# Layer 2's raw attention weights issued on ScalarE's queue instead of SyncE's

## The chip, the core and the metric

The kernel runs on one core of a Trainium2 chip. A core has five engines that run their own instruction streams in order: TensorE (PE, with its weight loads shown as PEld), VectorE (DVE), ScalarE (ACT), GpSimd (POOL) and SyncE (SP), which computes nothing here and only issues transfers. ACT and POOL can issue transfers as well. The metric is the time of one execution on the device in microseconds (us); the kernel before took 1427.58 us in the median of three runs (1425.8 to 1429.04).

## The reference

Four layers work on x of shape (4, 256, 256); each adds a cross-attention and then a feed-forward part to x, both on a layer-normalised copy. All is in float32. What bears on this change is the end of layer 1 and the beginning of layer 2.

Layer 1's feed-forward part is a mixture of experts. Each of the 1024 tokens picks two of eight experts, and a shared expert runs for all tokens:

```python
    scores = jax.nn.softmax(logits, axis=-1)
    topk_w, topk_idx = jax.lax.top_k(scores, K)
    ...
    g = jax.nn.silu(jnp.einsum('th,efh->tef', x, w_gate)) * jnp.einsum('th,efh->tef', x, w_up)
    expert_out = jnp.einsum('tef,ehf->teh', g, w_down)
    y = jnp.einsum('te,teh->th', cw, expert_out).reshape(b, s, h)
    y = y + _swiglu_mlp(x, sw_gate, sw_up, sw_down).reshape(b, s, h)
```

Layer 2's attention has 16 query heads of 128 over 8 key and value heads, with weights Wq (256, 2048), Wk and Wv (128, 1024) and Wo (2048, 256):

```python
    q = (text_hidden @ Wq).reshape(B, T_text, N_HEADS, HEAD_DIM).transpose(0, 2, 1, 3)
    k = (vision_tokens @ Wk).reshape(B, T_vis, N_KV_HEADS, HEAD_DIM).transpose(0, 2, 1, 3)
    v = (vision_tokens @ Wv).reshape(B, T_vis, N_KV_HEADS, HEAD_DIM).transpose(0, 2, 1, 3)
    ...
    return out @ Wo
```

## The kernel before

The program is one straight line of instructions. Inside a stretch marked `manual_schedule`, PE, ACT, DVE and POOL take their instructions in the order of the source. SP's instructions, nearly all transfers, are put in order by the planner.

**Layer 1's experts.** Tokens are sorted by expert into 23 blocks of 128 slots (`NBLK`). The loop at lines 2464 to 2492 is a pipeline over these blocks, three deep. For block j it does, on the engines in brackets:
- `gather` [POOL]: bring the block's 128 token rows from `xd` in HBM into `xg` by an indirect transfer; there are four buffers, so POOL runs up to four blocks ahead.
- `turn_in` [PE, ACT]: transpose into PSUM (`pxg`, L2344), then ACT copies to `xgT` (L2346).
- `weights` [DVE]: copy the expert's weights into `we`.
- `rise` [PE, ACT, DVE]: twelve matmuls into `pgu` (L2369), two Silu on ACT into `sg` (L2374, L2375), two products on DVE into `gT` and `gR`.
- `fall` and `last_rows` [PE]: matmuls into `pyr` (L2387, L2393).
- `store` [ACT, SP]: ACT scales `pyr` into the result tile `yr` (L2398); SP then stores `yr` to `yd` in HBM, 128 KB (L2401). There are three `yr` buffers, so the `yr` of block j can be written only when the store of block j - 3 has landed.

Blocks go in pairs: `last_rows` and `store` of both are done in the odd iteration. On ACT the two `yr` are followed by the next iteration's `xgT`, its two `sg`, another `xgT` and two more `sg`, and then the next two `yr`.

After the loop the tokens' results are gathered back from `yd` by POOL (L2410).

**Layer 2's folding.** Before layer 2's attention the weights are folded: Wq with Wk, and Wv with Wo, in eight steps (`folding`, matmuls `pm` at L985 and `pn` at L1001), two for each of four groups of raw weights. A group is four transfers, 512, 128, 128 and 512 KB (`load_raw`, L969). They are issued within the block loop, after blocks 1, 5, 9 and 13. The first group goes into parts of the folded weights' own tiles that are written last (so the profile calls these transfers `n_sb` and `m_sb`), the other three into tiles of a pool with three buffers. `done["slots"]` is the last `yr` instruction; `behind` makes the load wait for it:

```python
    dma = nc.sync.dma_start(dst, src[a * P : (a + z) * P, :].rearrange("(h e) d -> e h d", e=P))
    if after:
        behind(dma, after)
```

SP's order in the loop is so: the stores of two blocks, a group of four loads, the stores of two blocks and two more, a group of loads, and so on. Layers 1 and 3 load their raw weights by the same function, with SP as the issuer.

Of the kernel before, what the change touches and what calls it, by code (L numbers as in the profile page):

```python
# [17 lines left out]
P = 128  # L18
# [817 lines left out]
def bounded_path(ctx: ExitStack, tc: tile.TileContext, t, out: bass.AP, over):  # L836


    nc = tc.nc
# [38 lines left out]
    def behind(dma, ins):  # L878

        tc.add_manual_dep(  # L880
            dma.ins, ins.name, mybir.DependencyInfo(mybir.DependencyClass.Sync, mybir.DependencyReason.DATA),
            reason="pace",
        )
# [71 lines left out]

    raws = {}

    def load_raw(L, i, after=None, tiles=None):

        wq, wk, wv, wo = (t[f"L{L}_{n}"] for n in ("wqT", "wkT", "wvT", "wo"))  # L960
        h0, g0 = 4 * i, 2 * i
        if tiles is None:
            tiles = [
                rawp.tile(shape, F32, tag=f"{n}_t", name=f"{n}_{L}_{i}")
                for n, shape in (("wq", [P, 4, D]), ("wk", [P, 2, DC]), ("wv", [P, 2, DC]), ("wo", [P, 4, D]))
            ]
        wq_t, wk_t, wv_t, wo_t = tiles
        for dst, src, a, z in ((wq_t, wq, h0, 4), (wk_t, wk, g0, 2), (wv_t, wv, g0, 2), (wo_t, wo, h0, 4)):
            dma = nc.sync.dma_start(dst, src[a * P : (a + z) * P, :].rearrange("(h e) d -> e h d", e=P))  # L969
            if after:  # L970
                behind(dma, after)
        raws[L, i] = wq_t, wk_t, wv_t, wo_t

    def folding(L, m_sb, n_sb):

        for i in range(4):
            h0 = 4 * i
            if (L, i) not in raws:
                load_raw(L, i)
            wq_t, wk_t, wv_t, wo_t = raws.pop((L, i))  # L980
            for g in range(2):
                pm = bank("mm", [P, ND, 2, DC], f"pm_{L}_{i}_{g}")
                for d in range(ND):
                    for h in range(2):
                        nc.tensor.matmul(  # L985
                            pm[:, d, h, :],
                            lhsT=wq_t[:, 2 * g + h, d * P : (d + 1) * P],
                            rhs=wk_t[:, g, :],
                            start=True,
                            stop=True,  # L990
                        )
                h1 = h0 + 2 * g
                nc.scalar.mul(m_sb[:, :, h1 : h1 + 2, :], pm, 1.0 / math.sqrt(P))
                m2 = rawp.tile([P, ND, 2, DC], F32, tag="m2", name=f"m2_{L}_{i}_{g}", bufs=1)
                for h in range(2):
                    nc.scalar.activation(
                        m2[:, :, h, :], m_sb[:, :, h1 + h, :], AF.Square,
                        accum_out=msq[:, L - 1, h1 + h : h1 + h + 1],
                    )
                pn = bank("mm" if "ring" in banks else "os"[g], [P, 2, D], f"pn_{L}_{i}_{g}")  # L1000
                nc.tensor.matmul(  # L1001
                    pn, lhsT=wv_t[:, g, :], rhs=wo_t[:, 2 * g : 2 * g + 2, :], start=True, stop=True
                )
                nc.vector.tensor_copy(n_sb[:, h1 : h1 + 2, :], pn)
                yield

    def folded(L):
        return (
            mnp.tile([P, ND, H, DC], F32, tag="m_sb", name=f"m_sb{L}"),
            mnp.tile([P, H, D], F32, tag="n_sb", name=f"n_sb{L}"),  # L1010
        )
# [7 lines left out]
    done = {}  # L1019
# [1148 lines left out]
    with tc.manual_schedule(engines={E.PE, E.Activation, E.DVE, E.Pool}):  # L2168
        back = ExitStack()
        backp = back.enter_context(tc.tile_pool(name="back", bufs=4, side="right"))  # L2170
        with tc.tile_pool(name="f1", bufs=2) as fp:
# [292 lines left out]
            for j in range(-2, NBLK + 1):  # L2464
                if j + 2 < NBLK:
                    if j + 2 >= 4:
                        blocks[j + 2].gather()
                    if j >= 0:
                        blocks[j + 2].weights()
                    blocks[j + 2].turn_in()  # L2470
                if 0 <= j + 1 < NBLK:
                    blocks[j + 1].rise()
                if 0 <= j < NBLK:
                    blocks[j].fall()
                    if j % 2 == 0 and j + 1 < NBLK:
                        blocks[j + 1].other_rows()
                    if j % 2 or j == NBLK - 1:
                        pair = blocks[j - j % 2 : j + 1]
                        for one in pair:
                            one.last_rows()  # L2480
                        for one in pair:
                            one.store()

                if j == 1:

                    mn = folded(2)
                    load_raw(
                        2, 0, done["slots"],
                        (mn[1][:, 8:12, :], mn[0][:, 1, 12:14, :], mn[0][:, 1, 14:16, :], mn[1][:, 12:16, :]),
                    )  # L2490
                if j in (5, 9, 13):
                    load_raw(2, j // 4, done["slots"])
            fold = folding(2, *mn)
            backs = {}
            shared[3].up([1, 2])
# [301 lines left out]
    with tc.manual_schedule(engines={E.PE, E.Activation, E.DVE, E.Pool}):  # L2797
# [124 lines left out]
    slots = late.tile([P, KSEL], F32, tag="slots", name="slots")  # L2922
    nc.gpsimd.iota(
        slots, pattern=[[1, KSEL]], base=1, channel_multiplier=0, allow_small_or_imprecise_dtypes=True
# [212 lines left out]
    with tc.manual_schedule(engines={E.PE, E.Activation, E.DVE, E.Pool}):  # L3137
# [34 lines left out]
        a, z = slice(0, P), slice(P, D)  # L3172
# [13 lines left out]
def tile_cross_attention_blocks(tc: tile.TileContext, t, out: bass.AP):  # L3186
    nc = tc.nc
    with tc.tile_pool(name="over", bufs=1) as pool:
        over = pool.tile([1, 1], I32, tag="over", name="over")
        again = bounded_path(tc, t, out, over)  # L3190
        with tc.If(again > 0):
            general_path(tc, t, out)
# [66 lines left out]
```

## Time and profile before

| what | value |
|---|---|
| median of three runs | 1427.58 us (1425.8 to 1429.04) |
| the profiled execution | 1426.74 us, of which the span is 1424.9 |
| granted clock of TensorE, mean | 0.997 |
| PE busy | 1401.6 us, 98% of the span |
| DVE, POOL, ACT busy | 896.7, 679.2, 590.2 us (63%, 48%, 41%) |
| SP's transfer queue | 37.29 MB in all |
| ACT's transfer queue | 1.31 MB: three loads at the start, two stores at the end |
| the block loop's pairs, undisturbed | 4.75 us |

The profile is of one execution. A row names the engine, the line of the source, what is written from what, and how long one instruction took; the idle time of the engine before it is given with what ended it. ACTq and SPq are the queues of an engine's own instructions that only issue transfers: the row's length is how long the issue held the engine's instruction stream, not how long the data took to land. In tables of stretches each engine's busy time in that stretch stands with its number of instructions.

### The profile page before, as it was taken

The numbers are of one execution on the slowest core, as the hardware profiler recorded it, in microseconds if no ns is written. First come the engines' busy times: TensorE is split into PE (matmuls) and PEld (weight loads), VectorE is DVE, ScalarE is ACT, GpSimd is POOL, SyncE is SP. The second block draws the span as 40 slices with busy tenths as digits, with TensorE's granted clock in tenths as the row PEclk, the third lists the DMA queues.
The fourth block names the chain that finished last, engine by engine and source line by source line (L and its number), as shares of the span: only waits on it lengthen the run. The fifth ranks groups of instructions, "written<-read, shape, count | busy, mean of one in ns | idle before, by whom it ended". The sixth has DMA issues, their size and how long they took to land. (4 is left out here: it accounts for less than half of the span.)

```text
span 1424.9 us, 20263 instructions
## 1 busy us (share of the span) xinstructions
PE 1401.6 (98%) x7393; PEld 927.0 (65%) x7393; DVE 896.7 (63%) x2012; ACT 590.2 (41%) x1168; POOL 679.2 (48%) x812
## 2 busy tenths in 40 slices
PE   9999999999999999999999999999999999999998
PEld 7566676566556667887555666665985556666666
DVE  6666863666665557554676565648755666575675
ACT  5667454433433332255443333333454433333331
POOL 3322332475655455231566656566214765445560
PEclk9999999999999999999999999999999999999999
DMA  5000220300000000272120000000331000000000
GB/s 163 2 1 2 75 75 1 86 27 1 8 0 8 1 8 22 53 217 91 49 56 8 16 1 1 8 1 9 117 106 48 16 1 1 1 1 1 1 1 33
DMA packets 49449, 46.82 MB, mean 33 GB/s; under 512 B 8281, under 2 KB 45242, under 8 KB 49340
## 3 DMA queue, kind: packets, MB, share of 16 engines
q1 hardware_dynamic: 45740, 37.29, 8.6%
q0 software_dynamic: 2496, 6.82, 1.8%
q8 instruction: 61, 1.00, 0.3%
q10 hardware_dynamic: 1104, 1.31, 0.3%
q14 instruction: 48, 0.39, 0.1%
HBM read 38.60 MB, written 6.82 MB: 32 GB/s over the span
## 5 line engine op out<-in xcount | busy, mean ns | idle before, releaser
L1870 POOL TENSOR_TENSOR half<-pT 128x1024 f32<-128x1024 f32 x93 | 218.2, 2347 | 290.7 <-ACT pT L1854 215.6
L1851 PE MATMUL ps<-qT,cT 128*128 128x512 f32 x768 | 345.6, 593 | 0.0
L1859 PE MATMUL po<-pT,c_sb 128*128 128x512 f32 x768 | 345.3, 592 | 0.0
L1854 ACT ACTIVATE pT<-ps,mbias 128x512 f32<-128x512 f32 x384 | 263.7, 687 | 155.9 <-PE ps L1851 141.6
L1859 PEld LDWEIGHTS po<-pT,c_sb 128*128 128x128 f32 x768 | 145.8, 190 | 183.2 <-issue 183.2
L1851 PEld LDWEIGHTS ps<-qT,cT 128*128 128x128 f32 x768 | 138.9, 190 | 138.4 <-issue 136.5
L1863 ACT COPY oT<-po 128x512 f32<-128x512 f32 x96 | 56.2, 586 | 265.0 <-PE po L1859 265.0
L1906 POOL TENSOR_TENSOR oT<-oT,wide 128x512 f32<-128x512 f32 x90 | 114.3, 1290 | 17.3 <-DVE wide L1905 17.3
L1831 DVE TENSOR_TENSOR qT<-qT,paq 128x128 f32<-128x128 f32 x90 | 25.4, 283 | 94.9 <-ACT qT L1830 94.9
L1344 ACT ACTIVATE pT<-ps 128x512 f32<-128x512 f32 x128 | 65.9, 604 | 32.6 <-PE ps L1340 32.4
L1878 DVE TENSOR_TENSOR half<-half 128x512 f32<-128x512 f32 x96 | 71.6, 746 | 2.7 <-POOL half L1868 2.5
L1831 DVE TENSOR_TENSOR w<-w,pao 128x128 f32<-128x128 f32 x21 | 6.0, 286 | 106.5 <-ACT w L1830 106.5
L1880 DVE STREAM_TRANSPOSE turned<-half 128x512 f32<-128x512 f32 x96 | 68.3, 712 | 6.3
L1821 PE MATMUL paq<-xnT_a,m_sb 128*128 128x128 f32 x360 | 71.3, 280 | 0.0
L1821 PE MATMUL paq<-xx,m_x 128*128 128x128 f32 x360 | 69.6, 275 | 0.0
L1821 PEld LDWEIGHTS paq<-xnT_a,m_sb 128*128 128x128 f32 x360 | 57.3, 192 | 17.2 <-issue 8.7
L1884 DVE TENSOR_REDUCE sums<-turned 128x16 f32<-128x512 f32 x96 | 65.9, 686 | 3.3
L1821 PE MATMUL pao<-n_x,ox 128*128 128x128 f32 x336 | 65.2, 276 | 0.3 <-POOL ox L1747 0.3
L1830 ACT COPY qT<-paq 128x128 f32<-128x128 f32 x90 | 23.9, 265 | 94.1 <-PE paq L1821 94.1
L1905 DVE STREAM_TRANSPOSE wide<-rz 128x512 f32<-128x512 f32 x96 | 62.2, 685 | 0.1
L1834 DVE TENSOR_TENSOR qT<-qT,pbq 128x384 f32<-128x384 f32 x90 | 49.9, 554 | 9.4
L1821 PEld LDWEIGHTS paq<-xx,m_x 128*128 128x128 f32 x360 | 54.7, 192 | 0.0
(454 smaller groups left out, 2589.2 us busy)
## 6 DMA issues: line engine op xcount, KB each, us to landing
wq<-in_L_wqT SPq DMA_DIRECT2D x11, 512.0 KB, 5.1
wo<-in_L_wo SPq DMA_DIRECT2D x11, 512.0 KB, 7.4
yd<-yr SPq DMA_DIRECT2D x23, 128.0 KB, 4.9
w<-in_F_w SPq DMA_DIRECT2D x4, 512.0 KB, 3.6
xd<-xn_f SPq DMA_DIRECT2D x7, 256.0 KB, 2.2
wk<-in_L_wkT SPq DMA_DIRECT2D x11, 128.0 KB, 5.2
wv<-in_L_wvT SPq DMA_DIRECT2D x11, 128.0 KB, 5.6
x_sb<-in_x SPq DMA_DIRECT2D x4, 256.0 KB, 3.1
```

The costliest lines, as they stand in the source:

```text
L1344: nc.scalar.activation(pT[kp][:, j], ps[j], AF.Exp)
L1821: nc.tensor.matmul(p[:, at, :], lhsT=lhsT, rhs=rhs, start=(k == 0 and at == 0), stop=(k == len(of) - 1 and i == which[-1]),)
L1851: nc.tensor.matmul(ps, lhsT=cT[:, b, k * P : (k + 1) * P], rhs=qT, start=True, stop=True)
L1854: nc.scalar.activation(pT[:, k, :], ps, AF.Exp, bias=mbias[:, b, k : k + 1])
L1859: nc.tensor.matmul(po, lhsT=c_sb[:, b, k, :], rhs=pT[:, k], start=(k == 0), stop=(k == NK - 1))
L1863: done["head"] = nc.scalar.copy(raw, po).ins
L1870: nc.gpsimd.tensor_tensor(half, pT[:, 0:2], pT[:, 2:4], ALU.add)
L1878: nc.vector.tensor_tensor(part, half[:, 0], half[:, 1], ALU.add)
L1880: nc.vector.transpose(turned.rearrange("p f i -> p (f i)"), part)
L1884: nc.vector.tensor_reduce(sums[b, hp // 4][:, hp % 4, :], turned, AX.X, ALU.add)
L1905: nc.vector.transpose(wide, rzs[b, hp // 4][:, hp % 4, :, None].to_broadcast([P, NB, 32]))
L1906: eng.tensor_tensor(outs[b, hp], outs[b, hp], wide.rearrange("p f i -> p (f i)"), ALU.mult)
```

## The change

`load_raw` gets a parameter for the queue that issues its transfers. The four calls in layer 1's block loop, which bring layer 2's raw weights, pass ScalarE; other callers still get SyncE. The transfers themselves, their tiles and the tie to the last `yr` are as before. Since ACT takes its instructions in the order of the source, a group's four issues now stand on ACT behind the two `yr` of blocks 0 and 1 (4 and 5, 8 and 9, 12 and 13) and ahead of the next `xgT`. The stores of `yr` stay on SP.

```diff
-    def load_raw(L, i, after=None, tiles=None):
+    def load_raw(L, i, after=None, tiles=None, queue=None):
...
-            dma = nc.sync.dma_start(dst, src[a * P : (a + z) * P, :].rearrange("(h e) d -> e h d", e=P))
+            dma = (queue or nc.sync).dma_start(dst, src[a * P : (a + z) * P, :].rearrange("(h e) d -> e h d", e=P))
             if after:
                 behind(dma, after)
...
                 if j == 1:
 
                     mn = folded(2)
                     load_raw(
                         2, 0, done["slots"],
                         (mn[1][:, 8:12, :], mn[0][:, 1, 12:14, :], mn[0][:, 1, 14:16, :], mn[1][:, 12:16, :]),
+                        queue=nc.scalar,
                     )
                 if j in (5, 9, 13):
-                    load_raw(2, j // 4, done["slots"])
+                    load_raw(2, j // 4, done["slots"], queue=nc.scalar)
```

## The prediction

> **What bounds the kernel now.** I read the page's slices first, then the busy time of each engine pair by pair of blocks in the stage that the change touches, then the timeline of that stage.
>
> The page (part 2, one digit for each fortieth of the span):
>
> ```profile
> PE   9999999999999999999999999999999999999998
> ACT  5667454433433332255443333333454433333331
> PEclk9999999999999999999999999999999999999999
> ```
>
> PE is busy over 90% in nearly every slice at its full clock, so a us in which PE stands still inside a stage is a us of the span, and nothing later waits for a fixed time that could swallow it. ACT is half idle on average, which says nothing about one moment. The chain that ended last is followed back only to 1060.8 us, behind this stage, so for the stage itself I go by stretches and waits.
>
> Stretches of two blocks each (us and, in brackets, instructions of PE, PEld, DVE, ACT, POOL; then the clock, the DMA share and GB/s):
>
> ```profile
> 607.20:611.95 4.75, 4.75 (x38) 3.98 (x36) 2.59 (x7) 2.56 (x8) 1.91 (x2) 1.00 0.57 123
> 611.95:616.70 4.75, 4.75 (x38) 3.98 (x36) 2.59 (x7) 2.56 (x8) 1.91 (x2) 1.00 1.03 340
> ...
> 635.70:641.40 5.70, 5.00 (x38) 4.01 (x36) 2.54 (x7) 2.57 (x8) 1.91 (x2) 1.00 0.59 142
> 641.40:646.15 4.75, 4.75 (x38) 3.98 (x36) 2.53 (x7) 2.56 (x8) 0.97 (x1) 1.00 0.86 257
> 646.15:652.53 6.38, 5.01 (x38) 4.01 (x36) 2.53 (x7) 2.57 (x8) 0.00 (x0) 1.00 0.38 127
> ```
>
> A pair takes 4.75 us when nothing disturbs it, and PE fills all of it. Two pairs are longer: 5.70 (+0.95) and 6.38 (+1.63). These 2.58 us are all that this stage loses to waits between pairs. The timeline shows why (start, length, engine, line; idle before and its releaser in brackets):
>
> ```profile
> 638.04 0.47 ACT L2398 ACTIVATE yr<-pyr,wslot 128x256 f32<-128x256 f32 x1 [1.75 <-DMA yd<-yr]
> 638.41 0.36 ACT L2346 COPY xgT<-pxg 128x256 f32<-128x256 f32 x1
> 638.83 1.59 PE L2369 MATMUL pgu<-xgT,we 128*128 128x128 f32 x12 [0.70 <-ACT xgT L2346]
> 649.17 0.47 ACT L2398 ACTIVATE yr<-pyr,wslot 128x256 f32<-128x256 f32 x1 [2.43 <-DMA yd<-yr]
> 649.54 0.36 ACT L2346 COPY xgT<-pxg 128x256 f32<-128x256 f32 x1
> 649.96 1.59 PE L2369 MATMUL pgu<-xgT,we 128*128 128x128 f32 x12 [1.37 <-ACT xgT L2346]
> ```
>
> ACT wants to write a result tile yr (three buffers) whose earlier store to yd has not landed. Queued behind it on ACT is the copy xgT, and PE's next pgu needs that. The late stores were issued behind raw weights on the same queue: stores issued at 631.6 and 642.0 took 6.2 and 6.6 us to land, those at 652.7 and 657.7, with no load ahead, 1.8 and 1.7.
>
> These two rows also give a law. The pairs begin (first pxg) at 635.72 and 646.17; xgT starts 2.69 and 3.37 us later, and the pair is 0.95 and 1.63 longer. So a pair loses (start of xgT after the pair's start) minus 1.74 us. In the undisturbed pair at 607.23 xgT starts at 608.06, 0.83 in: ACT has 0.91 us of slack there and no more.
>
> **Part 1, removed: sixteen load issues from SP.** The rows of the first and last group:
>
> ```profile
> 608.71 0.45 SPq L969 DMA_DIRECT2D n_sb<-in_L_wqT  x1
> 609.21 0.54 SPq L969 DMA_DIRECT2D m_sb<-in_L_wkT  x1
> 609.79 0.47 SPq L969 DMA_DIRECT2D m_sb<-in_L_wvT  x1
> 610.30 0.47 SPq L969 DMA_DIRECT2D n_sb<-in_L_wo  x1
> ...
> 638.91 0.60 SPq L969 DMA_DIRECT2D wq<-in_L_wqT  x1
> 639.57 0.50 SPq L969 DMA_DIRECT2D wk<-in_L_wkT  x1
> 640.12 1.16 SPq L969 DMA_DIRECT2D wv<-in_L_wvT  x1
> 641.32 0.61 SPq L969 DMA_DIRECT2D wo<-in_L_wo  x1
> ```
>
> From first start to last end the four groups hold SP for 2.06, 2.02, 2.77 and 3.02 us. Nothing computes on SP, so their removal alone saves nothing; what it may save is the two waits for stores, 2.58 us. I take all of it. The next store pair is issued one pair later, 612.58 against 608.71 for the first load; four issues on ACT will begin 0.4 us earlier than on SP and the pair itself grows by some 1.5 us, so the store comes up to 2 us later relative to the load, with less of the load in front of it. In the last group the gain is larger still: there SP's loads came 3.2 us into the pair, because they stood behind the stalled store, and on ACT they start 1 us in. From below: if a store still takes 6.6 us beside loads, the relief can be 0. A row near that end is the gathers xg, which have POOL's queue to themselves and still land in 3.7 to 6.8 us beside loads, against 2.8 without. But yr has to wait only when a store takes longer than about one pair plus 0.3 us (the 5.1 us landing of the store at 612.6 cost ACT 0.20 and PE nothing), and pairs with loads get longer.
>
> [...]
>
> **Part 2, added: the same sixteen issues on ACT, four at a time, right behind the two yr of a pair.** Behind them on ACT stand xgT, the two sg and the next xgT; PE waits for xgT, DVE's gT for sg. They begin when the second yr has ended, since they are tied to it: 0.95 us into the pair, plus 0.04 as between yr and its store on SP now. The trace shows three issues on ACT of another shape at the start and two at the end:
>
> ```profile
> L865 SPq DMA_DIRECT2D c_sb<-in_ctx x3: 390/409/427, 6.4 to 9.0; - x3
> L865 ACTq DMA_DIRECT2D c_sb<-in_ctx x1: 465/465/465, 0.8 to 0.8; - x1
> ```
>
> Same shape, 0.465 on ACT against 0.409 on SP; the two out stores have medians 0.552 and 0.512. I take ACT as 1.1 times SP. An undisturbed group is 2.04 on SP, so 2.25 on ACT. The two longer groups had 0.7 and 0.95 us more, each with one wv issue of about 1.2 us. I don't see its cause; on ACT's queue no stores stand ahead, so I take half, 2.6 and 2.7. Bounds: below, SP's 2.04 for all; above, 3.02 for all.
>
> By the law, with xgT 0.02 after the last issue, a group of length X costs PE 0.99 + 0.02 + X - 1.74 = X - 0.73 us: 1.52, 1.52, 1.87, 1.97, in all 6.9 us. The breakeven against the 2.58 is X = 1.38, or about 0.31 us an issue; every one of the sixteen rows on SP is 0.38 or more.
>
> **Part 3, moved past.** The stores keep SP's order among themselves and go out no later. POOL's gathers run two pairs ahead (9.5 us) and landed in 6.8 at most: covered by 2.7 us; without that cover pxg would wait. The folding begins at 662.5 with the first group and reaches the fourth at about 676; the last load, issued by about 640 on ACT with at most 7.7 us to landing, is there by 648. If that cover were gone, PE's pm would wait. In the built program of before, each transfer also waits for the one eight issues earlier; for a load that is the load of the group before, two pairs (9.5 us and more) earlier against 7.7: nothing, but on ACT such a wait would hold the whole chain.
>
> **Sum.** +6.9 - 2.58 = +4.3 us. The profiled execution took 1426.74 (span 1424.9 and 1.84 around it) and would take 1431.0; it stood 0.84 below the median of the runs, so for the median I say 1427.58 + 4.3 = 1431.9. A measurement of this kernel can tell about 0.2%, 2.86 us, from no change: the borders are 1424.7 and 1430.4.
>
> **The rivals.**
> - *Issues off PE's path (not slower).* Place: ACT between the second yr and xgT. ACT idles some 2.2 us of each pair, and if four issues took less than 1.38 us there the change would pay; below 0.73 us they cost nothing and the 2.58 are pure gain: 1425.0. Against it: sixteen rows of 0.38 and more. 10 in 100.
> - *Early start.* If the issues needn't wait for the end of the second yr but follow its start (0.48 in, 0.47 earlier), the undisturbed groups cost 1.05 each: 4.2 - 2.58 = +1.6, 1429.2. For it: xgT now starts before the second yr has ended. Against it: the loads are tied to that instruction's completion. 13 in 100.
> - *Long issues.* Every group holds ACT for 3.02 us as the fourth did SP: 4 x 2.29 - 2.58 = +6.6, 1434.2. 14 in 100.
> - *Stores no faster.* The two stalls stay although the queue is their own, as for the gathers: +6.9, 1434.5. 8 in 100.
> - *My forecast*, 55 in 100: from groups of 2.04 (4 x 1.31 - 2.58 = +2.7) to groups of 2.25, 2.25, 3.0 and 3.3, with the full excess (7.9 - 2.58 = +5.3): 1430.3 to 1432.9 as its own range.
>
> Slower by over 0.2%: the forecast but for its lowest edge (0.51) and the two last rivals (0.22), 0.73. Within: that edge (0.04), the early start (0.13) and half of the first rival (0.05), 0.22. Faster by over 0.2% needs a little more than the whole 2.58 us: the other half, 0.05. The range leaves out the first rival, at 1425.0, and a tail above the last two: 1428.5 to 1435.
>
> **What would show it.** Right: ACT issues of 0.4 to 0.6 us in four groups behind yr; the four pairs with loads 6.2 to 6.8 us long, with pgu waiting for xgT about 1.4 us; no ACT wait for yd in the pairs that were 5.70 and 6.38 (the second back at 4.75); stores landing in under 5 us. Wrong: pairs with loads still at 4.75 (issues hidden), a yr still waiting for yd (stores no faster), ACT issues of 1 us (long issues), or a pm that waits for a raw weight.

## The result and the profile after

The changed kernel took 1434.35 us in the median of five runs (1432.61 to 1434.69), the kernel before 1427.58 in five runs beside it (1425.80 to 1429.75): a ratio of 1.004, 95% interval 1.0028 to 1.0051. The profiled execution took 1434.67 us, its span 1432.9, at a mean granted clock of 0.995 against 0.997 before.

The slices of the page say nothing of it: PE is at 9 in all but the last, and the granted clock reads as before:

```profile
PEclk9999999999999999999999999999999999999999
```

The stretches of two blocks, in the columns of before (length; busy us of PE, PEld, DVE, ACT, POOL with their instructions; clock, DMA share, GB/s):

```profile
611.06:617.25 6.19, 5.02 (x39) 4.02 (x37) 2.59 (x8) 2.58 (x8) 1.91 (x2) 1.00 0.70 197
...
643.89:650.40 6.51, 5.02 (x38) 4.02 (x37) 2.58 (x8) 2.58 (x8) 1.91 (x2) 1.00 0.75 201
...
655.15:659.90 4.75, 4.75 (x39) 3.99 (x37) 2.54 (x8) 2.57 (x8) 0.00 (x0) 1.00 0.21 66
```

The first, third, fifth and seventh pair, those with a group of loads, are 1.44, 1.46, 1.45 and 1.76 us longer than 4.75. The others are undisturbed, the ninth (655.15) too, which lost 1.63 before. The timeline of the first and the last group (start, length, engine; idle before and its releaser in brackets):

```profile
611.16 0.84 ACT L2398 ACTIVATE yr<-pyr,wslot 128x256 f32<-128x256 f32 x2 [0.45 <-PE pyr L2393]
612.03 0.41 ACTq L969 DMA_DIRECT2D n_sb<-in_L_wqT  x1
612.49 0.58 ACTq L969 DMA_DIRECT2D m_sb<-in_L_wkT  x1
613.11 0.56 ACTq L969 DMA_DIRECT2D m_sb<-in_L_wvT  x1
613.71 0.48 ACTq L969 DMA_DIRECT2D n_sb<-in_L_wo  x1
614.23 0.37 ACT L2346 COPY xgT<-pxg 128x256 f32<-128x256 f32 x1 [2.22 <-PE pxg L2344]
614.65 1.59 PE L2369 MATMUL pgu<-xgT,we 128*128 128x128 f32 x12 [1.17 <-ACT xgT L2346]
...
645.32 0.98 ACTq L969 DMA_DIRECT2D wk<-in_L_wkT  x1
...
647.81 1.60 PE L2369 MATMUL pgu<-xgT,we 128*128 128x128 f32 x12 [1.49 <-ACT xgT L2346]
```

ACT is not computing between yr and xgT, but it is not free: the four issues fill 612.03 to 614.19. The bracket on xgT, "2.22 <-PE pxg", names the wrong releaser: pxg was there at 611.5, and the issues are what came last. From first start to last end the groups hold ACT for 2.16, 2.17, 2.17 and 2.47 us, the last because one wk issue took 0.98.

What ACT waited for ahead of the 23 yr, in the answer for that tile (us, times), first after, then before:

```profile
  PE pyr L2393: 5.2, 11
  issue: 1.1, 1
```

```profile
  DMA yd<-yr: 4.6, 4
```

The waits for stores, 4.6 us in four places before, are gone; what is left is PE's own pyr and one gap of 1.1 us that stands in both. How long each store took to land is not given in the changed kernel's traces; that no yr waited says that every store was in time.

**The account of the two traces.** From the first pxg of block 0 to the first pm of the folding it is 55.29 us before (607.23 to 662.52) and 58.80 after (611.06 to 669.86): +3.51, which is the 6.11 us that the four pairs are longer, less the 2.60 us that the two no longer lose. Yet the two spans differ by 8.0. Of the rest, 3.83 us was there when block 0 began, ahead of anything the change touches (607.23 against 611.06), and about 0.6 came behind the last matmul. The clock column, third from the end, shows where most of the 3.83 is from, in the stretch 40 to 60 us; before, then after:

```profile
40.00:60.00 20.00, 17.44 (x224) 11.18 (x220) 15.99 (x36) 14.41 (x29) 4.01 (x7) 1.00 0.01 2
```

```profile
40.00:60.00 20.00, 17.44 (x203) 11.30 (x202) 16.90 (x37) 12.98 (x26) 3.58 (x6) 0.91 0.01 2
```

PE is as busy in both, but at a clock of 0.91 instead of 1.00 over 20 us; from 586 to 600 it is 0.76 instead of 0.88. That is 1.8 and 1.7 us of full clock missing. Whether that belongs to the change was the first question to the chip.

### The profile page after: what moved, and what is told of

Read it like the earlier page. It is cut to its first block, busy times and chain, and to the rows that moved or that the text cites. A ratio compares the mean times of both kernels' runs of the same rounds, so it can differ in the third digit from the quotient of the medians.

```text
span 1432.9 us, 20265 instructions
## 1 busy us (share of the span) xinstructions
PE 1405.9 (98%) x7393; PEld 930.5 (65%) x7393; DVE 897.2 (63%) x2012; ACT 591.3 (41%) x1168; POOL 679.9 (47%) x812
```

## The experiments

Beside the times, each run is read by two numbers that the clock elsewhere does not touch: the lengths of its pairs, and the *loop* from block 0's first pxg to the first pm. With every pair at 4.75 the loop is 52.69 us; what a kernel has above that it has lost there.

**The changed kernel again** (no edit).

> The changed kernel once more, unaltered. Its profile put +3.5 us into the block loop (four pairs with loads at 6.19, 6.21, 6.20, 6.51 instead of 4.75, and 2.58 us of waits for stores gone), but it measured +6.8 in the medians. Theory 'clock': the rest is time in which TensorE's clock was granted at half, ahead of the loop, where the instruction streams of the engines are the same; then the loop adds +3.5 again, and what is over varies with the granted clock: a run of clock 0.997 would take about 1431. Rival 'change': the rest belongs to the change; then the total is +6 to +7 again at any clock, and some stretch behind the loop is longer by 3 us.

Measured: 1431.36 us in the median of seven runs (1430.49 to 1434.57) against 1427.23; ratio 1.0034 (1.0018 to 1.0051). The stretch again:

```profile
40.00:60.00 20.00, 17.43 (x224) 11.08 (x220) 16.36 (x36) 14.42 (x29) 4.03 (x7) 1.00 0.01 2
```

The clock is that of the kernel before (and 586 to 600 has 0.88), and block 0 begins at 607.62, 0.39 later than before. Its pairs with loads take 6.16, 6.37, 6.16 and 6.23, the others 4.75; the loop is 58.62. So of the 3.8 us ahead of the loop 3.4 were one execution's clock, and the loop's loss of 6 us (6.11, here 5.93) is the kernel's own.

**Load issues spread on ACT**, one behind each of the next four xgT instead of four in a row.

```diff
+            if later is None:
+                issue()
+            else:
+                later.append(issue)
...
+            slots_left = []
...
                     blocks[j + 2].turn_in()
+                if slots_left:
+                    slots_left.pop(0)()
...
-                        queue=nc.scalar,
+                        queue=nc.scalar, later=slots_left,
```

> The sixteen loads stay on ACT, but one issue stands behind each xgT instead of four behind the second yr, so that they fall into ACT's idle time ahead of sg (0.65 us in the even blocks, 1.01 in the odd ones, against issues of 0.41 to 0.58). Theory 'place': ACT's hold costs only because it stands ahead of xgT; all pairs take 4.75, the +6.1 us of the four long pairs go and the relief of 2.58 stays: 2.6 us below before, 1425.0 (6 below the changed kernel). Rival 'issue': an issue on ACT slows its neighbours wherever it stands (transfers issued there, sixteen times 0.4 us): 1431 or more.

Measured: 1426.20 (1424.37 to 1427.99), ratio 0.9992 (0.9981 to 1.0002). The first issue in ACT's timeline, behind the xgT of 608.65, and the stretch of its pair:

```profile
608.79 0.41 ACTq L970 DMA_DIRECT2D n_sb<-in_L_wqT  x1
```

```profile
607.82:612.57 4.75, 4.75 (x39) 3.99 (x37) 2.83 (x9) 2.56 (x8) 2.08 (x2) 1.00 0.61 190
```

All pairs are 4.75 and the loop is 52.69. The same sixteen issues on the same queue cost PE nothing where each stands in a gap of ACT, so it is the place of the issues, four in a row ahead of xgT, that costs 6 us. No yr waits for a store either.

**Loads on SyncE as before, results in more buffers.** From block 2 on, yr is one of eight slices of a tile that is idle until the folding.

```diff
-                    yr = fp.tile([P, D], F32, tag="yr", name=f"yr{j}", bufs=3)
+                    if j < 2:
+                        yr = fp.tile([P, D], F32, tag="yr", name=f"yr{j}", bufs=3)
+                    else:
+                        yr = mn[0][:, 0, 2 * (j % 8) : 2 * (j % 8) + 2, :].rearrange("p h c -> p (h c)")
```

> The kernel before, with loads on SP, but results from block 2 on are written to eight places in a tile that is idle in the loop (the folded weights' m_sb) instead of three yr tiles. It measures the relief alone. Theory: no yr waits for a store, the pairs of 5.70 and 6.38 become 4.75, and the time falls by 2.6 us to 1425.0. Rival 'late next': the stores' delay shows up elsewhere (the gathers of the results behind the loop wait for the last store) and the gain is under 1 us.

Measured: 1425.61 (1424.31 to 1428.73), ratio 0.9993 (0.9981 to 1.0004); all pairs 4.75, loop 52.68. The pair that took 6.38 before:

```profile
645.20:649.95 4.75, 4.75 (x39) 3.99 (x37) 2.54 (x8) 2.56 (x8) 0.00 (x0) 1.00 0.53 155
```

So the waits for stores are all that the kernel before loses in the loop, and more buffers remove them as fully as the change does.

**The changed kernel without the tie to the last yr.**

```diff
-                        2, 0, done["slots"],
+                        2, 0, None,
...
-                    load_raw(2, j // 4, done["slots"], queue=nc.scalar)
+                    load_raw(2, j // 4, queue=nc.scalar)
```

> The changed kernel, but the loads are not tied to the end of the second yr; their place on ACT is the same. Theory 'early start' as a size: the first issue begins at the second yr's start plus 0.1, some 0.4 us earlier, and each of the four pairs is 0.4 us shorter (about 5.8 instead of 6.2): 1.7 us below the changed kernel. Rival: an issue waits for the running activation anyway and nothing changes (within 0.5 us of the changed kernel).

Measured: 1430.43 (1427.23 to 1433.34), ratio 1.0021 (1.0010 to 1.0032). ACT's timeline at the first group, and at the last pair:

```profile
607.39 0.47 ACT L2398 ACTIVATE yr<-pyr,wslot 128x256 f32<-128x256 f32 x1 [0.45 <-PE pyr L2393]
607.44 0.39 ACTq L969 DMA_DIRECT2D n_sb<-in_L_wqT  x1
...
651.03 0.47 ACT L2398 ACTIVATE yr<-pyr,wslot 128x256 f32<-128x256 f32 x1 [2.15 <-DMA yd<-yr]
```

The issues now start 0.05 us after the first yr, beside the two activations, and a group costs 0.54, 1.24 (its wk issue was slow), 0.64 and 0.60. But a wait for a store is back: the yr at 651.03 needs the store of a yr that ended at 644.1, which so took some 7 us to land, although it had SyncE's queue to itself. That pair lost 1.36. The loop is 57.09. The rival fell, since the issue of 607.44 did not wait for the activation that ran from 607.39. And the own queue did not ensure that a store was in time when the loads ran beside it; it is one store in this trace, the others were in time.

**Six useless copies on ACT instead of the issues**, behind the second yr of blocks 5, 9 and 13; loads on SyncE, results in seven slices as above.

```diff
+                if j in (5, 9, 13):
+                    for _ in range(6):
+                        nc.scalar.copy(mn[0][:, 0, 14:16, :].rearrange("p h c -> p (h c)"), blocks[j].xgT.rearrange("p d t -> p (d t)"))
```

> The loads stay on SyncE and results have their own slices (as in sp_yr8: all pairs 4.75 us, median 1425.61), and ACT instead makes six useless copies of 128x256 behind the second yr of blocks 5, 9 and 13, three pairs in all. Theory 'hold' (a pair loses whatever keeps ACT beyond its slack, transfers have nothing to do with it): with copies of 0.33 to 0.37 us, 2.0 to 2.2 us in all, xgT starts 3.0 to 3.2 us into the pair and each of the three pairs loses 1.25 to 1.45 us: pairs of 6.0 to 6.2, loop +3.8 to +4.4 over sp_yr8, 1429.4 to 1430.0 us. Rival 'transfers' (the long pairs of the changed kernel came from loads and gathers colliding when ACT issues them): pairs stay 4.75 to 4.95 and the time at 1425.6 to 1426.2.

Measured: 1431.27 (1428.19 to 1434.98), ratio 1.0017 (1.0004 to 1.0030). The six copies of the second of the three pairs, and the stretch of the first:

```profile
629.99 2.58 ACT L2489 COPY m_sb<-xgT 128x256 f32<-128x256 f32 x6
```

```profile
618.08:624.41 6.33, 5.01 (x39) 4.01 (x37) 2.59 (x8) 4.79 (x14) 1.92 (x2) 1.00 0.71 203
```

The copies took 2.58 us, more than the 2.0 to 2.2 I had expected, and xgT starts 3.32 us into the pair; 3.32 - 1.74 = 1.58, and the three pairs are 6.33 or 6.34, the others 4.75. The loop, 57.45, lies above the expected range because the copies took longer, and the time does too. Work that moves no data over a queue costs what the issues cost: the hold of ACT is the cause, not the transfers.

**Each load in two halves**, eight issues in a group.

```diff
+            for k in range(2 if queue else 1):
+                n = z // 2 if queue else z
+                dma = (queue or nc.sync).dma_start(dst[:, k * n : (k + 1) * n], part[:, k * n : (k + 1) * n])
```

> The changed kernel with each load cut into two halves: the same bytes, eight issues in a group on ACT instead of four, the first behind the second yr. Theory 'hold per issue': 0.4 to 0.55 us an issue, 3.2 to 4.4 us a group, xgT 4.2 to 5.4 us into the pair, each of the four pairs loses 2.5 to 3.6 us, that is +1.0 to +2.2 over the changed kernel's 1.45; loop +4.2 to +8.7 over the changed kernel, 1435.6 to 1443 us. Rival 'hold per byte' (an issue's length goes with the rows it describes, so halves take half the time): group 2.2 us, pairs 6.2, 1431 to 1432 us as in act_again.

Measured: 1447.35 (1446.80 to 1450.25), ratio 1.0131 (1.0109 to 1.0152), above the range of either theory. The halves take as long to issue as whole loads (eight in 4.01 us at the first group, four whole loads in 2.16), so the hold goes by issues and not by bytes. xgT starts 5.02 us into that pair, which by the law costs 3.28; the pair, 609.92 to 619.58, lost 4.91. Two stretches of it, with the clock third from the end, and PE's row show the rest:

```profile
609.92:615.20 5.28, 2.42 (x20) 2.08 (x18) 0.83 (x2) 1.10 (x3) 1.91 (x2) 1.00 0.66 181
...
616.20:617.20 1.00, 1.00 (x6) 1.00 (x6) 0.94 (x3) 0.00 (x0) 0.00 (x0) 0.50 1.06 367
```

```profile
615.37 2.50 PE L2372 MATMUL pgu<-xgT,we 128*128 128x128 f32 x12 [3.03 <-ACT xgT L2349]
```

PE stood still for 3.03 us, and then its granted clock was halved for 3.4 us: twelve matmuls took 2.50 instead of 1.59. The four groups lost 4.91, 7.35, 4.95 and 5.83, of which 3.28, 5.08, 3.36 and 3.55 follow from the start of xgT. The other 7.8 us, and 0.39 in the pair behind the fourth group, fall into stretches at 0.50, which last 3.4, 6.8, 3.4 and 6.8 us. The loop is 76.14.

**Loads spread on SyncE.** Each load is tied to one of the next four xgT; SyncE then issues two stores, two loads, two stores, two loads. ACT issues nothing. Against the kernel with the loads spread on ACT:

```diff
-                    behind(dma, after)
+                    behind(dma, after if later is None else done["xgT"])
...
-                    nc.scalar.copy(self.xgT, pt)
+                    done["xgT"] = nc.scalar.copy(self.xgT, pt).ins
...
-                        queue=nc.scalar, later=slots_left,
+                        later=slots_left,
...
-                    load_raw(2, j // 4, done["slots"], queue=nc.scalar, later=slots_left)
+                    load_raw(2, j // 4, done["slots"], later=slots_left)
```

> The loads are spread as in act_spread but stay on SyncE: one load tied to each of the next four xgT, so that SyncE's order is two stores, two loads, two stores, two loads. ACT issues nothing. Theory 'spacing' (act_spread lost its store waits because at most two loads stand between stores; the queue is not what counts): no yr waits for a store for longer than 0.3 us, all pairs 4.75 to 4.8, loop -2.4 to -2.6 against before, 1425.0 to 1426.0 us. Rival 'own queue' (stores need a queue without loads): stores behind a 512 KB load land in over 5.5 us, yr waits in at least two pairs, loop -1.0 to +1.0, 1426.5 to 1428.5 us.

Measured: 1426.14 (1424.20 to 1428.69) against 1428.48, ratio 0.9986 (0.9974 to 0.9997). SyncE's timeline, and what ended most of ACT's waits ahead of the 23 yr (beside it there is only 1.1 us of "issue"):

```profile
617.12 0.46 SPq L970 DMA_DIRECT2D m_sb<-in_L_wvT  x1
618.46 0.38 SPq L970 DMA_DIRECT2D n_sb<-in_L_wo  x1
620.95 0.81 SPq L2407 DMA_DIRECT2D yd<-yr  x2
```

```profile
  PE pyr L2399: 5.0, 11
```

No wait for a store, every pair 4.75, loop 52.69. The stores issued behind two loads were all in time; in the first trace of before, the four pairs of stores issued behind four loads took 4.7 to 6.6 us to land. With loads and stores on one queue and two loads between the stores, the stores are in time: spacing alone brings the relief, without a second queue.

**The kernel before, two more traces.** In the six runs so far with whole loads, the changed kernel's second among them, the differences of the medians to before were 0.3 to 1.6 us less favourable than those of the loops (the loads spread on ACT gained 1.0 us, and in the loop 2.6), which made me doubt the 2.6.

> The kernel before once more, for a second trace of its block loop. Theory 'the relief is a steady 2.6 us': two long pairs, 0.7 to 1.9 us each, 2.2 to 3.0 us in all, each with an ACT wait for a store before yr. Rival 'the relief varies from run to run' (it is the landing time of a store behind loads): anything from 0 to 4 us, and a mean below 2 would account for some 1 us of the medians' difference that the traces do not show.

> The same a third time: by 'steady' 2.2 to 3.0 us again in the loop; by 'varies' a sum that differs from the others by over 0.8 us.

Measured (one execution each): 1424.19 and 1428.28 us. The longest of ACT's waits for stores in the second trace, then the two longest in the third:

```profile
646.73 0.47 ACT L2398 ACTIVATE yr<-pyr,wslot 128x256 f32<-128x256 f32 x1 [1.08 <-DMA yd<-yr]
```

```profile
631.49 0.47 ACT L2398 ACTIVATE yr<-pyr,wslot 128x256 f32<-128x256 f32 x1 [2.25 <-DMA yd<-yr]
650.59 0.47 ACT L2398 ACTIVATE yr<-pyr,wslot 128x256 f32<-128x256 f32 x1 [0.91 <-DMA yd<-yr]
```

The four waits stand at the same pairs each time as in the first trace (the other three of the second trace are 0.53, 0.97 and 0.60, the other two of the third 0.38 and 0.37), but their sizes change, and PE feels only what is beyond 0.80 us of a wait (1.08 cost it 0.29, 2.25 cost 1.45), so its loss changes more: 2.60, 0.47 and 1.56 us in the three traces (loops of 55.29, 53.16 and 54.25), 1.54 in the mean. "Steady" fell.

## Why the prediction was right, and where it was not

**The account over all runs.** Single times swing with the granted clock. A fit over the 126 runs of seven kernels (all but the halves), with a constant for each kernel and one slope for the clock, says that a run is 1.11 us (± 0.15) longer for each 0.001 that its mean clock is lower. It gives these differences to the kernel before at equal clock (with 95% intervals), which stand beside what the loops of the traces say with the mean loss of 1.54:

| kernel | loss in its loop | less 1.54 | by the fit |
|---|---|---|---|
| the change (two traces, 12 runs) | 6.11, 5.93 | +4.5 | +5.2 ± 0.7 |
| without the tie | 4.40 | +2.9 | +2.4 ± 0.7 |
| six copies | 4.76 | +3.2 | +3.2 ± 0.7 |
| spread on ACT | 0.00 | -1.5 | -1.4 ± 0.8 |
| spread on SyncE | 0.00 | -1.5 | -1.5 ± 0.7 |
| more buffers | -0.01 | -1.5 | -1.2 ± 0.8 |

The loops and the times agree, for the change only at the edge of the interval. The +6.8 us between the first two medians is this +5.2 and, by the slope, 0.8 for the clock: the first five runs of the change had 0.9944 in the mean, the 56 runs of before 0.9951. The clocks of the five runs of before beside them were not recorded, so the other 0.8 us stays open.

**Part 1, the store relief.** Predicted: both long waits go, 2.58 us. The waits did go, in both traces of the changed kernel. But the sentence "I take all of it" took one execution's stalls for the kernel's: three traces give 1.54 in the mean, and by the fit the three kernels that lose nothing in the loop are 1.2 to 1.5 us ahead. This term was mis-sized by about 1.0 us, and the two rows it came from could not show that. The trace did hold a warning that I used only for something else: a stall is the landing time less a threshold, and landings of 5.1 to 6.6 us lay on both sides of it.

Its reason was half right. I expected relief from the queue and from the longer pairs. The run without the tie had the own queue and still a store of 7 us; the loads spread on SyncE had no own queue and no late store. An own queue alone was neither enough nor needed here.

**Part 2, the issues on ACT.** The law, loss = start of xgT in the pair less 1.74, holds to 0.01 us: xgT started 3.17, 3.19, 3.18 and 3.49 into the pairs, giving 1.43, 1.45, 1.44 and 1.75 against 1.44, 1.46, 1.45 and 1.76 measured; it also gives the copies (1.58) and the first untied group (2.27 - 1.74 = 0.53 against 0.54). The size of X was a little high: 2.16, 2.17, 2.17 and 2.47 where I took 2.25, 2.25, 2.6 and 2.7. The step that failed is "I take half" of the excess of SyncE's two longer groups. That excess is one slow issue now and then (0.98 here, 1.19 and 1.16 in the first trace of before, 1.42 with the loads spread on SyncE, 2.72 for two wk issues of the halves; none above 0.66 in the second and third trace of before). It stood in the second, third or fourth group, never in the first, and its cause stays open; half of it in both later groups was too much. The term came to 6.1 and 5.9 instead of 6.9.

**The sum.** 6.9 - 2.58 = +4.3 was predicted; 6.0 - 1.5 = +4.5 is what the traces give now. Two terms were each about 1 us too large, and they cancelled. That was luck: the number was better than its parts. Nor could the time alone have shown that the mechanism was right. The first median, 1434.35, lies above the forecast's own 1430.3 to 1432.9 and beside two rivals, 1434.2 for *long issues* and 1434.5 for *stores no faster*; the second, 1431.36, lies inside. It is the traces that rule the two out for this kernel: groups of 2.16 to 2.47 us instead of 3.02, and no yr that waited for a store.

**Part 3, moved past.** Nothing there came due: no pm waited for a raw weight, no pxg for a gather, and no issue on ACT stood waiting for the one before.

**The rivals.** *Issues off PE's path*: refuted in this place, true of another, as the spread on ACT shows. *Early start*: it needs the tie removed; then the issues start earlier still and a group costs less than the 1.05 I priced (0.54, 0.64 and 0.60 in the three groups without a slow issue), but a store wait comes back. *Long issues*: one of sixteen reached 0.98. *Stores no faster*: not in the changed kernel, but for one store in the kernel without the tie. That the changed kernel's longer pairs are what kept its stores in time fits all runs, but was not tried alone.

**A version below both kernels.** Three of these, the loads spread on ACT, spread on SyncE, and the larger set of result buffers, take the 52.69 us loop. Against the kernel before they are some 1.5 us ahead, about 0.1%; only the spread on SyncE has an interval that ends below 1 (0.9997).

## What to carry to other kernels

Before moving transfers to an engine that computes, look up what stands behind them in its order and how much slack that has: it is the number of issues in a row that counts (here about 0.54 us each against 0.9 us of slack), so put them singly where the engine waits anyway. The late stores were cured by letting them in between the loads, or made harmless by more result buffers (seven or eight were tried); another queue was not needed for that, and once not enough. And a stall that is "landing time less a threshold" should be read from several traces before it enters a sum, since one trace may hold the largest.

## What the runs showed of the hardware that I had not expected

- **A standstill of PE of 3 us cost more than itself.** With eight issues PE idled 3.03 to 3.30 us in three groups, and 4.83 in the one with the 2.72 us of wk issues. Its granted clock was then 0.50 for about 3.4 us in the first and third group and for about 6.8 in the second and fourth, in these two partly while PE still stood, which added 1.6 to 2.7 us to each. The stalls of 1.17 to 1.49 us in the changed kernel's first and last group left the clock at 1.00. The moment of the fall, worked out from the clock column, differs: in the first group (0.84 from 615.20 to 616.20) about 615.9, half a us after PE had begun again at 615.37; in the fourth (0.72 from 655.62 to 666.20) about 660.3, some 2.2 us after PE's last matmul had ended at 658.04 and 1 us before the next. What sets the moment and the length is not shown here.
- **The clock ahead of the loop differed between executions of one kernel.** The changed kernel began block 0 at 611.06 us in one execution and at 607.62 in the next, nearly all of it by its clock; no edit tried here but the changed kernel's hold and the halves moved the time by more. The kernel before varies too: in its three traces block 0 begins at 607.23, 606.92 and 609.68.
- **An untied issue started beside ACT's arithmetic.** At 607.44 one began 0.05 us after a yr of 0.47 us, and the next yr started on time, at 607.76; tied to the yr's end, the first issue of the changed kernel waited for both (612.03, behind the two yr of 611.16 to 612.00).
